# A top-2 mixture-of-experts block on one core: the first expert's second weights in two loads, a reordered front with unmarked row numbers, and seven output buffers for the pairs at the end

## The chip, the core and the metric

One core of a Trainium2 chip runs the whole computation in one launch. The metric is the device time in microseconds (us) of one execution. TensorE is called PE here (PEld is its weight load), VectorE DVE, ScalarE ACT, GpSimd POOL, SyncE SP.

## The reference

The input x has 64 x 64 = 4096 tokens of 256 numbers. Each token is routed to 2 of 8 experts, an expert is a network of three layers, and the weighted sum of its two experts' outputs is added to the token. The gate reads the normed token and a second input per batch row.

```python
var = jnp.mean(x * x, axis=-1, keepdims=True)
xn = rms_w * (x * jax.lax.rsqrt(var + EPS))
gate = xn @ wg_W + wg_b + (genre_embed @ gg_W + gg_b)
gate_w = jax.nn.softmax(gate, axis=-1)
topk_w, topk_i = jax.lax.top_k(gate_w, TOP_K)
cw = jnp.sum(jax.nn.one_hot(topk_i, E, dtype=x.dtype) * topk_w[..., None], axis=-2)
h1 = jax.nn.relu(jnp.einsum('bsh,ehm->bsem', x, W1) + b1)
h2 = jax.nn.relu(jnp.einsum('bsem,emn->bsen', h1, W2) + b2)
out_e = jnp.einsum('bsen,enh->bseh', h2, W3) + b3
x = x + jnp.einsum('bseh,bse->bsh', out_e, cw)
```

E = 8, W1 is 256 x 512, W2 512 x 512 and W3 512 x 256 for each expert, all in float32.

## The kernel before, in words

**The sparse plan.** Only the chosen pairs of token and expert are computed. The pairs of one expert are cut into tiles of 128 rows. POOL fetches the tokens of a tile by number with an indirect DMA, and adds the finished rows to the output by number with another (line 1481, a scatter). A token has two pairs, so a unit's scatters wait until those of the unit before have landed.

**The front.** The first 8 of every 32 tokens (part A) are gated first, so that seven first tiles, one for each of the first seven experts (F = 7), can start early. `first_part` turns tokens with PE (`turn`, `turn_pe` and a copy out of PSUM), multiplies them by the gate's weights (`gates`, `gates_2`), picks the two best experts (`choose`), ranks the pairs, and builds the table of rows `tabA` with one-hot products. A line of DVE turns it into row numbers: `idxA` holds the token's number, and 4096 (a mark beyond the last row) where a tile has an empty place, so that an empty place fetches and writes nothing. `other_loads` issues the loads of the next experts on SP, behind the first gather of rows on POOL. `second_part` goes on with the gate of the other 24 of 32 tokens (part B): more turning, `gates(1, range(4, 8))` with the copy to `gTs` and its turn back (`upright`), then the turn of the first tile's rows (`transpose_x(0)`, line 958, with its copy to `xT`, line 959). Between these stand sums of squares for the norms (`squares`, lines 238 and 240), shared out to ACT and DVE; DVE's come by `some(n)`.

**The head.** `head_step` runs the seven first tiles: layer 1 (line 1090), its relu (1093), layer 2 (1102, 1105), layer 3 (1442). Between its products it finishes the gate of part B (`third_part`, `last_upright`, `norm`, `ranks_of_rest`), plans the rest of the work in `rest()` on DVE, and builds the second table of rows, `idxR`, with 64 one-hot products (`table`, line 649). Row numbers of part B then let POOL gather the rows of the later units.

**The units.** The later tiles are grouped into units of one expert: 4 tiles, 3 tiles or 2 tiles (pairs). Layers 1 and 2 are done by a scheme that takes seven block products in place of eight (class `Fast`, line 1191), layer 3 likewise (`Wide` and, for 3 and 2 tiles, `Duo`, line 1379). Which groups there are is read from the data and picks one of the arms written out beforehand. In the profiled data, nine units of four tiles, four of three and six pairs follow the head. Layer 3 of a unit runs inside the step of the unit behind it, woven into that unit's layers 1 and 2 by hand.

**Outputs.** A unit's finished rows stand in `ys`, 4 buffers of 128 x 256. `y_of` names the buffer: a unit of three or four tiles begins at slot 0, a pair takes slots 0 and 1 or 2 and 3 in turn. ACT (line 1393) and DVE (line 1395) write the quarters of a pair's two buffers in the order ACT, DVE, DVE, ACT, and `send` issues the scatter. A buffer can be written again only when its scatter has landed. The ring `xg` (3 buffers) takes the first tiles' rows, and serves no one after the head but for two outputs.

**Order.** The program is in program order on each engine (a manual schedule): an engine whose next instruction waits holds all behind it. SP's loads are one queue, POOL's gathers and scatters are another.

Of the kernel before, what the change touches and what calls it, by code (L numbers as in the profile page):

```python
# [54 lines left out]
def kernel(  # L55
# [17 lines left out]
    nc = tc.nc  # L73
# [121 lines left out]

    idxA = const.tile([P, E], I32, name="idxA")
    idxR = const.tile([P, NREST], I32, name="idxR")
    ebt = const.tile([P, 1], I32, name="ebt")
# [121 lines left out]
    class Part:  # L320
# [31 lines left out]
        def norm(self, root):  # L352


            var, y, t = (self.t[a] for a in ("var", "y", "t"))
            if root:
                nc.scalar.activation(t, ss[:, self.i0 : self.i1], AF.Sqrt, bias=epsb)
            V.scalar_tensor_tensor(var, ss[:, self.i0 : self.i1], H * EPS, fresh[:, 0, 1:2].to_broadcast([P, self.n]), ALU.add, ALU.add)
            if root:
                V.reciprocal(y, t)  # L360
            else:
                V.tensor_scalar(t.bitcast(I32), var.bitcast(I32), 1, None, ALU.arith_shift_right)
                V.tensor_scalar(y.bitcast(I32), t.bitcast(I32), -1.0, float(0x5F3759DF), ALU.mult, ALU.add)
            n = 1 if root else 3
            for k in range(n):
                V.scalar_tensor_tensor(t, y, -0.5, var, ALU.mult, ALU.mult)
                V.tensor_tensor(t, t, y, ALU.mult)
                V.scalar_tensor_tensor(self.t["rstd"] if k == n - 1 else y, t, 1.5, y, ALU.add, ALU.mult)

        def choose(self, raw, add):  # L370
# [105 lines left out]

    squares_late = []
    left = [NA + i for i in (0, 1, 4, 5, 2, 3, 6, 7)] + list(range(NA + 8, NI))

    def some(n):  # L480
        for _ in range(n):
            squares(left.pop(0), "V")

    def first_part():
# [15 lines left out]
        V.memset(cw8B, 0.0)  # L500
        for k in range(3):
            V.memset(ring(run, [P, H], "xg", 3, k), 0.0)
        V.memset(cgR, 0.0)
# [22 lines left out]
        nc.sync.dma_start(vecs[E * MC : 2 * E * MC, :], b2.rearrange("e (c p) -> (e c) p", p=P))  # L526
        load_weights(0, (0, 1))
        gates_2(((0, 1), (2, 3)), PB[3], ((0, 0), (0, 1), (1, 0), (1, 1)))
# [51 lines left out]
        turn_pe(j0, 0, 3, [TPB - 1])  # L580
        turn_copy(8, "A", 3)
        V.tensor_scalar(sa[:, 0:E], tabA, 0.0, float(NT), ALU.is_equal, ALU.mult)
        V.scalar_tensor_tensor(idxA, tabA, float(OFFA), sa[:, 0:E], ALU.add, ALU.add)
        V.tensor_copy(totA1, pA.tot)
        some(3)

    def other_loads():

        sent = nc.gpsimd.memset(shut, 0.0)

        load_weights(1, (0,))
        tc.add_manual_dep(
            loads[2].ins,
            sent.ins.name,
# [10 lines left out]
    def second_part():  # L605

        j0 = GA + 4
        vps = PB[6][:, 384 : 384 + 2 * E * MC]
        gates(1, range(4, 8))
        nc.scalar.copy(gTs, PB[3])  # L610
        turn_pe(j0, 1, 0)
        turn_pe(j0 + 1, 0, 4)
        turn_copy(9, "A", 0)
        turn_copy(10, "V", 4)
        pA.weights()
        raw = upright(PB[2])
        nc.scalar.copy(graw[:, NA : NA + 4 * TPB, :].rearrange("p (q k) e -> p q k e", q=4), raw)
        turn_pe(j0 + 1, 1, 1)
        turn_copy(11, "A", 1)
        nc.tensor.transpose(vps, vecs, ident[: 2 * E * MC, : 2 * E * MC])  # L620
        V.tensor_copy(vT.rearrange("p l e c -> p (l e c)"), vps)
        gates_2(((8, 9), (10, 11)), PB[7], ((0, 0), (1, 0)))
        squares(left.pop(), "A")
        squares(left.pop(), "A")
        transpose_x(0)
        squares(left.pop(), "A")
        gates_2(((8, 9), (10, 11)), PB[7], ((0, 1), (1, 1)))
        squares_late.extend((left.pop(), left.pop()))
        some(6)

    def third_part():

        nc.scalar.copy(gTs[:, 0:HT], PB[7][:, 0:HT])
        some(len(left))

    def last_upright():
# [256 lines left out]

    def fetch(dst, src, b):

# [3 lines left out]
            in_=src,  # L899
            in_offset=bass.IndirectOffsetOnAxis(ap=index(b), axis=0),  # L900
            bounds_check=NT - 1,
# [10 lines left out]
    def gather(b):  # L912
        fetches.append(fetch(ring(run, [P, H], "xg", 3, b), xrows, b))

# [355 lines left out]
    def y_of(u, k):  # L1270
        if F - 2 <= u < F:
            return ring(run, [P, H], "xg", 3, u + 2)
        return ys[:, slots(u).start + k]

# [250 lines left out]
    def head_step(u):  # L1525
# [3 lines left out]
        for k in range(3 * u, min(3 * u + 3, F)):  # L1529
            gather_cw(k)  # L1530
        layer1(u, {1: ranks_of_rest} if u == 2 else None)
        if u == 0:
# [6 lines left out]
            squares(squares_late.pop(), "A")  # L1539
            layer2(u, {0: lambda: squares(squares_late.pop(), "A"), 1: last_upright, 2: lambda: transpose_x(1)})  # L1540
            stage_1(1)
# [10 lines left out]
        if u == 4:  # L1552
            until("chunk0")
            spread_high[0](2)
            table(GC)
            until("chunk1")
# [15 lines left out]
        elif u == 4:  # L1572
            table(2 * GC)
            until("chunk3")
            layer2(u, {1: lambda: table(3 * GC), 2: table})
        else:
# [431 lines left out]
```

## Time and profile before

| what | value |
|---|---|
| time, median of 3 runs | 441.06 us (439.86 to 442.34) |
| the profiled execution's own time | 441.69 us |
| its span from first to last instruction | 440.0 us |
| PE busy | 431.8 us, 98% |
| DVE, ACT, POOL busy | 350.5, 267.0, 276.6 us |
| mean granted TensorE clock | 0.998 |
| bytes moved by DMA | 96.99 MB, 220 GB/s |

The chain of the work that ended last is 91% PE. Such a kernel is read from PE's idle time: the view of who waited for whom lists the waits of PE, and the table by windows shows in which stretches PE was not busy. A row of the timeline gives the start, the length, the engine, the line and the operation, and in brackets the idle time ahead of it and what ended it. In the view by windows each engine has its busy time and the number of its instructions. In the chain, a row gives start, length and what the time went to.

### The profile page before, as it was taken

To read this page: it belongs to the slowest core of one execution; us is meant where nothing else is said; L and a number is where in the kernel's file an instruction comes from. 1 tells how busy PE (TensorE), PEld (TensorE's weight loads), DVE (VectorE), ACT (ScalarE), POOL (GpSimd) and SP (SyncE) were. 2 spreads that over 40 slices of the span, in tenths; PEclk is the share of its full clock that TensorE was granted. 3 is DMA by queue.
4 is the path that set the end of the run, shared out by engine and by line. 5 is a ranking of instruction groups with operands and counts; after the bars stand their busy time and mean duration, and the time that the engine had idled before them with its cause. 6 is when DMAs were issued, how large, how long until landed. Compare 5 with 4: busy or idle time off the path is not lost.

```text
span 440.0 us, 9508 instructions
## 1 busy us (share of the span) xinstructions
PE 431.8 (98%) x3085; PEld 409.3 (93%) x3085; DVE 350.5 (80%) x894; ACT 267.0 (61%) x787; POOL 276.6 (63%) x233
## 2 busy tenths in 40 slices
PE   9999999999999999999999999999999998999995
PEld 8699999889898999989999999999999998999995
DVE  6899974797868787786868697877877887999982
ACT  6855834646474746565564747475575678577772
POOL 6866335778888767474848483848666677655233
PEclk9999999999999999999999999999999999999999
DMA  8999999899986586674748392939688678878413
GB/s 312 339 345 408 368 324 318 224 334 275 361 199 131 115 230 151 195 170 147 196 127 234 96 253 67 265 93 334 183 256 221 186 210 264 231 242 243 99 20 51
DMA packets 85903, 96.99 MB, mean 220 GB/s; under 512 B 36079, under 2 KB 64850, under 8 KB 85716
## 3 DMA queue, kind: packets, MB, share of 16 engines
q1 hardware_dynamic: 49472, 40.54, 29.0%
q10 hardware_dynamic: 21188, 38.29, 25.6%
q0 software_dynamic: 15184, 17.47, 20.6%
q8 instruction: 26, 0.43, 0.4%
q14 instruction: 33, 0.27, 0.2%
HBM read 80.68 MB, written 20.20 MB: 229 GB/s over the span
## 4 chain that ended last, share of the span: by engine, by line
PE 91%; DMA 5%; issue 2%; DVE 1%; POOL 0%; ACT 0%; POOLq 0%; DVEq 0%
PE pb L1191 56%; PE pb L1320 13%; PE pb L1102 6%; PE pb L1379 5%; DMA out_dram<-ys,idxR 3%; PE pb L1090 3%; PE pb L1442 2%; PE pb L1401 1%; PE pb L649 1%; PE pb L317 1%; DMA xg<-in_x_dram,idxA 1%; PE pb L249 1%; DMA big<-out_dram,idxR 1%; PE pb L280 0%; PE pb L958 0%
## 5 line engine op out<-in xcount | busy, mean ns | idle before, releaser
L1481 POOL DMA_INDIRECT out_dram<-ys,idxR x60 | 99.2, 1654 | 80.8 <-DVE ys L1467 37.3
L896 POOL DMA_INDIRECT cg<-cwdR,idxR x60 | 67.3, 1121 | 18.3 <-issue 17.1
L1248 ACT ACTIVATE hid<-hid,bb 128x256 f32<-128x256 f32 (+9 forms) x158 | 63.4, 451 | 9.3 <-DVE hid L1210 4.4
L1248 ACT ACTIVATE hid<-pb,bb 128x128 f32<-128x128 f32 (+9 forms) x146 | 53.0, 416 | 24.5 <-PE pb L1191 23.5
L1191 PE MATMUL pb<-hid,w2r 128*128 128x128 f32 (+9 forms) x304 | 56.0, 327 | 0.0
L1191 PE MATMUL pb<-hotA,big 128*128 128x128 f32 (+9 forms) x304 | 52.8, 327 | 0.0
L1191 PEld LDWEIGHTS pb<-hotA,big 128*128 128x128 f32 x304 | 47.7, 191 | 2.8
L1191 PEld LDWEIGHTS pb<-hid,w2r 128*128 128x128 f32 x304 | 47.6, 191 | 2.4
L1191 PE MATMUL pb<-mixX,iotx 128*128 128x128 f32 (+9 forms) x228 | 46.5, 327 | 0.0
L896 POOL DMA_INDIRECT xgE<-in_x_dram,idxR x32 | 34.3, 1071 | 18.8 <-DVE ib L827 9.3
L1191 PEld LDWEIGHTS pb<-mixX,iotx 128*128 128x128 f32 x228 | 36.6, 191 | 1.9
L1202 ACT COPY big<-pb 128x256 f32<-128x256 f32 (+9 forms) x39 | 18.8, 483 | 30.4 <-PE pb L1191 29.9
L896 POOL DMA_INDIRECT big<-in_x_dram,idxR x28 | 31.8, 1137 | 8.5 <-issue 7.0
L1200 ACT COPY pb<-pb 128x256 f32<-128x256 f32 (+9 forms) x36 | 16.5, 459 | 25.9 <-PE pb L1191 25.7
L1191 PE MATMUL pb<-xT,w1r 128*128 128x128 f32 (+9 forms) x152 | 31.1, 327 | 0.0
L951 DVE STREAM_TRANSPOSE xT<-gTs 128x256 f32<-128x256 f32 x56 | 29.6, 635 | 0.0
L1191 PE MATMUL pb<-mixB,w2r 128*128 128x128 f32 (+9 forms) x152 | 28.0, 327 | 0.0
L1191 PE MATMUL pb<-mixB,big 128*128 128x128 f32 (+9 forms) x152 | 28.0, 327 | 0.0
L1191 PE MATMUL pb<-hid,big 128*128 128x128 f32 (+9 forms) x152 | 28.0, 327 | 0.0
L1202 ACT COPY q1s<-pb 128x256 f32<-128x256 f32 (+9 forms) x39 | 18.8, 482 | 14.4 <-PE pb L1191 14.4
L1102 PE MATMUL pb<-hid,w2r 128*128 128x128 f32 x224 | 27.3, 276 | 0.0
L1102 PEld LDWEIGHTS pb<-hid,w2r 128*128 128x128 f32 x224 | 26.5, 192 | 0.3
(369 smaller groups left out, 1012.3 us busy)
## 6 DMA issues: line engine op xcount, KB each, us to landing
w2r<-in_L_cond_W_dram ACTq DMA_DIRECT2D x17, 1024.0 KB, 8.7
w2r<-in_L_cond_W_dram SPq DMA_DIRECT2D x9, 1024.0 KB, 12.9
w3r<-in_L_cond_W_dram ACTq DMA_DIRECT2D x17, 512.0 KB, 4.3
w1r<-in_L_cond_W_dram ACTq DMA_DIRECT2D x16, 512.0 KB, 7.5
w1r<-in_L_cond_W_dram SPq DMA_DIRECT2D x10, 512.0 KB, 9.7
w3r<-in_L_cond_W_dram SPq DMA_DIRECT2D x9, 512.0 KB, 11.0
big<-in_x_dram SPq DMA_DIRECT2D x8, 512.0 KB, 5.5
gTs<-scr SPq DMA_DIRECT2D x8, 512.0 KB, 4.7
```

The costliest lines, as they stand in the source:

```text
L896: return nc.gpsimd.indirect_dma_start(out=dst, out_offset=None, in_=src, in_offset=bass.IndirectOffsetOnAxis(ap=index(b), axis=0), bounds_ ...
L951: V.transpose(xT[:, :, s0 + k, :].rearrange("p c (b k) -> p k c b", b=SQ), shs[:, s0 + k].rearrange("p k (a c) -> p k c a", a=SQ),)
L1090: nc.tensor.matmul(ph, lhsT=w1[:, c, ts(m, P)], rhs=cols[:, c, :], start=(c == 0), stop=(c == HC - 1))
L1102: nc.tensor.matmul(ph, lhsT=w2[:, m, ts(n, P)], rhs=hid[0][:, m, 0:BT], start=(m == 0), stop=(m == MC - 1))
L1191: nc.tensor.matmul(bank[:, ts(n, self.w)], lhsT=w[:, c, ts(n, P)], rhs=x[:, c], start=new and n == 0 and c == 0, stop=n == HB - 1 and c == ...
L1200: nc.scalar.copy(self.A, self.U)
L1202: nc.scalar.copy(self.q[(1, 6, 5).index(k)], self.tall(self.X if k == 5 else self.U))
L1248: nc.scalar.activation(out, src, AF.Relu, bias=ww[self.u][1][:, self.l, n : n + 1])
L1320: nc.tensor.matmul(bank[:, ts(j, H // 2)], lhsT=a[:, c, ts(j, P)], rhs=b[:, c], start=new and j == 0 and c == 0, stop=j == 1 and c == HB - ...
L1379: nc.tensor.matmul(bank, lhsT=a[:, c], rhs=b[:, c], start=False, stop=c == HB - 1, skip_group_check=True)
L1442: nc.tensor.matmul(sums(u, k), lhsT=hid[1][:, n, ts(k, BT)], rhs=w3[:, n, :], start=(i == 0), stop=(i == MC - 1))
L1481: add = nc.gpsimd.indirect_dma_start(out=orows, out_offset=bass.IndirectOffsetOnAxis(ap=index(b)[0:n], axis=0), in_=y[0:n], in_offset=None ...
```

## The change

It has three parts.

1. **W2 of the first expert** is loaded in two halves of its columns (`half_of_first`). The first half stands where the whole load stood. The second is issued in `other_loads` and waits for a new array of row numbers, `rowA`.
2. **Unmarked numbers and the front's order.** `rowA` is the table plus an offset, in integers, with no mark: an empty place of a tile fetches some token's row, which is never written out. The gathers of the first tiles use it in place of `idxA`; the scatters and the weights' gathers keep `idxA`. The three memsets of `xg` go. In `second_part` the turns and all gate products come ahead of the first rows' turn; the rows are turned into two PSUM banks, and ACT and DVE copy one half each to `xT`; the upright turn of the gate stands behind them. DVE's squares are dealt 1 + 2 + 6 in place of 3 + 6 ahead of the head, and one of ACT's squares moves into the head's first layer 2. `ranks_of_rest` moves behind the fourth product group of its layer 1, the first 16 one-hot products behind a layer 3, the last 16 behind the fourth group of a layer 2. `norm` carries `z = -0.5 * y * var` along, with the same number of operations.
3. **Seven buffers.** Outputs of the units of two and three tiles go round through the 3 buffers of `xg` and the 4 of `ys`.

```diff
     idxA = const.tile([P, E], I32, name="idxA")
+    rowA = const.tile([P, E], I32, name="rowA")
...
+            n, z = 1 if root else 3, self.t["den"]
+            V.scalar_tensor_tensor(z, y, -0.5, var, ALU.mult, ALU.mult)
             for k in range(n):
-                V.scalar_tensor_tensor(t, y, -0.5, var, ALU.mult, ALU.mult)
-                V.tensor_tensor(t, t, y, ALU.mult)
+                V.tensor_tensor(t, z, y, ALU.mult)
                 V.scalar_tensor_tensor(self.t["rstd"] if k == n - 1 else y, t, 1.5, y, ALU.add, ALU.mult)
+                if k < n - 1:
+                    V.scalar_tensor_tensor(z, t, 1.5, z, ALU.add, ALU.mult)
...
+    def half_of_first(k):
+        h = slice(k * M // 2, (k + 1) * M // 2)
+        return nc.sync.dma_start(w2r[0][:, :, h], W2[0].rearrange("(c p) n -> p c n", p=P)[:, :, h])
...
-        for k in range(3):
-            V.memset(ring(run, [P, H], "xg", 3, k), 0.0)
...
-        load_weights(0, (0, 1))
+        load_weights(0, (0,))
+        half_of_first(0)
...
+        found.append(V.tensor_scalar(rowA, tabA, float(OFFA), None, ALU.add))
         V.tensor_scalar(sa[:, 0:E], tabA, 0.0, float(NT), ALU.is_equal, ALU.mult)
...
-        some(3)
+        some(1)
...
+        later = half_of_first(1)
+        tc.add_manual_dep(
+            later.ins,
+            found[0].ins.name,
...
-        gates(1, range(4, 8))
-        nc.scalar.copy(gTs, PB[3])
         turn_pe(j0, 1, 0)
...
-        pA.weights()
-        raw = upright(PB[2])
-        nc.scalar.copy(graw[:, NA : NA + 4 * TPB, :].rearrange("p (q k) e -> p q k e", q=4), raw)
         turn_pe(j0 + 1, 1, 1)
         turn_copy(11, "A", 1)
         nc.tensor.transpose(vps, vecs, ident[: 2 * E * MC, : 2 * E * MC])
+        gates(1, range(4, 8))
+        gates_2(((8, 9), (10, 11)), PB[7], ((0, 0), (1, 0), (0, 1), (1, 1)))
+        squares(left.pop(), "A")
+        nc.scalar.copy(gTs, PB[3])
+        some(2)
         V.tensor_copy(vT.rearrange("p l e c -> p (l e c)"), vps)
-        gates_2(((8, 9), (10, 11)), PB[7], ((0, 0), (1, 0)))
+        pA.weights()
+        g = ring(run, [P, H], "xg", 3, 0).rearrange("p (r c) -> p c r", c=HC)
+        for c, (bank, eng) in enumerate(((PB[4], nc.scalar.copy), (PB[5], V.tensor_copy))):
+            nc.tensor.transpose(bank[:, 0:BT], g[:, c], ident)
+            eng(xT[:, c, 0, :], bank[:, 0:BT])
+        raw = upright(PB[2])
+        nc.scalar.copy(graw[:, NA : NA + 4 * TPB, :].rearrange("p (q k) e -> p q k e", q=4), raw)
         squares(left.pop(), "A")
-        squares(left.pop(), "A")
-        transpose_x(0)
-        squares(left.pop(), "A")
-        gates_2(((8, 9), (10, 11)), PB[7], ((0, 1), (1, 1)))
-        squares_late.extend((left.pop(), left.pop()))
+        squares_late.extend((left.pop(), left.pop(), left.pop()))
         some(6)
...
-        fetches.append(fetch(ring(run, [P, H], "xg", 3, b), xrows, b))
+        fetches.append(fetch(ring(run, [P, H], "xg", 3, b), xrows, b, rowA[:, b : b + 1]))
...
+        if u >= F and 1 < size(u) < SLOTS:
+            first = next(v for v in range(F, u + 1) if size(v) < SLOTS)
+            n = (turn_of(u, k) - turn_of(first, 0)) % (SLOTS + 3)
+            return ring(run, [P, H], "xg", 3, n) if n < 3 else ys[:, n - 3]
         return ys[:, slots(u).start + k]
...
-        layer1(u, {1: ranks_of_rest} if u == 2 else None)
+        layer1(u, {3: ranks_of_rest} if u == 2 else None)
...
             spread_high[0](2)
-            table(GC)
             until("chunk1")
...
-            layer2(u, {1: lambda: table(3 * GC), 2: table})
+            layer2(u, {1: lambda: table(3 * GC), 3: table})
```

**PE in the front, before.** From the last product of part A's table to the first products of the head. Rows with `big` turn tokens, rows with `wg_sb` are gate products, `gTs` is the gate's upright turn, `vecs` the biases' turn, `xg` the first tile's rows, `w1r` layer 1.

```order
L424 MATMUL pb_74<-incA,ones_105 128x9
L249 MATMUL pb_73<-ident,big 128x128
L265 MATMUL pb_71<-hid_93,wg_sb 32x512 x4
L249 MATMUL pb_68<-ident,big 128x128 x4
L249 MATMUL pb_72<-ident,big 128x128 x4
L299 MATMUL pb_70<-ident,gTs 128x128 x4
L249 MATMUL pb_69<-ident,big 128x128 x4
L620 MATMUL pb_74<-ident,vecs 128x64
L280 MATMUL pb_75<-q1s,wg_sb 32x256 x4
L958 MATMUL pb_72<-ident,xg_212 128x128 x2
L280 MATMUL pb_75<-q1s,wg_sb 32x256 x2
L280 MATMUL pb_75<-mixB,wg_sb 32x256 x2
```

The same stretch of PE now:

```order
L427 MATMUL pb_74<-incA,ones_105 128x9
L250 MATMUL pb_73<-ident,big 128x128
L250 MATMUL pb_68<-ident,big 128x128 x4
L250 MATMUL pb_72<-ident,big 128x128 x4
L250 MATMUL pb_69<-ident,big 128x128 x4
L629 MATMUL pb_74<-ident,vecs 128x64
L266 MATMUL pb_71<-hid_93,wg_sb 32x512 x4
L281 MATMUL pb_75<-q1s,wg_sb 32x256 x6
L281 MATMUL pb_75<-mixB,wg_sb 32x256 x2
L639 MATMUL pb_72<-ident,xg_381 128x128
L639 MATMUL pb_73<-ident,xg_381 128x128
L300 MATMUL pb_70<-ident,gTs 128x128 x4
```

The last four gate products moved ahead of the first rows' turn and the upright turn moved behind it; nothing was added or taken away.

**ACT in the front, before.** Its work from the two squares behind the exponents to the first relus of layer 1 (`hid`). `q1s` and `mixB` are turned tokens, `gTs` and `graw` the gate.

```order
L238 ACTIVATE sqA,ss<-big 128x256 x2
L260 COPY q1s<-pb_73 128x512
L610 COPY gTs<-pb_71 128x512
L260 COPY q1s<-pb_68 128x512
L617 COPY graw<-pb_70 128x128
L260 COPY mixB<-pb_69 128x512
L238 ACTIVATE sqA,ss<-big 128x256 x2
L959 COPY xT<-pb_72 128x2x128
L238 ACTIVATE sqA,ss<-big 128x256
L1093 ACTIVATE hid_93<-pb_68,vT 128x128
```

And now:

```order
L239 ACTIVATE sqA,ss<-big 128x256 x2
L261 COPY q1s<-pb_73 128x512
L261 COPY q1s<-pb_68 128x512
L261 COPY mixB<-pb_69 128x512
L239 ACTIVATE sqA,ss<-big 128x256
L633 COPY gTs<-pb_71 128x512
L640 COPY xT<-pb_72 128x128
L642 COPY graw<-pb_70 128x128
L239 ACTIVATE sqA,ss<-big 128x256
L1114 ACTIVATE hid_93<-pb_68,vT 128x128
```

The copy of the gate `graw` moved from ahead of the rows' copy to behind it, so a copy and a square stand between the rows and the first relu.

**POOL at the end, before.** From the first units of three tiles to the first pairs, in the arm that the profiled data takes. `out_dram<-` are the scatters, `<-in_x_dram` the gathers of rows, `cg` those of weights.

```order
L1481 DMA out_dram<-ys,idxR 4096x256 x3
L896 DMA big<-in_x_dram,idxR 128x256 x2
L896 DMA cg<-cwdR,idxR 128x8 x2
L1481 DMA out_dram<-ys,idxR 4096x256 x3
L896 DMA xgE<-in_x_dram,idxR 128x256 x2
L896 DMA cg<-cwdR,idxR 128x8 x2
L1481 DMA out_dram<-ys,idxR 4096x256 x2
```

The same stretch of POOL now (the last two units of three tiles, then the first pair):

```order
L1506 DMA out_dram<-ys,idxR 4096x256
L1506 DMA out_dram<-xg_381,idxR 4096x256
L1506 DMA out_dram<-xg_382,idxR 4096x256
L917 DMA big<-in_x_dram,idxR 128x256 x2
L917 DMA cg<-cwdR,idxR 128x8 x2
L1506 DMA out_dram<-xg_383,idxR 4096x256
L1506 DMA out_dram<-ys,idxR 4096x256 x2
L917 DMA xgE<-in_x_dram,idxR 128x256 x2
L917 DMA cg<-cwdR,idxR 128x8 x2
L1506 DMA out_dram<-ys,idxR 4096x256 x2
```

The order of the scatters is as it was; only the buffers that they read have changed, and the first pair's two no longer are those of the unit ahead of it.

More of the change, by code (lines that the diff above doesn't have):

```diff
@@ L363, in norm @@
                 V.tensor_scalar(y.bitcast(I32), t.bitcast(I32), -1.0, float(0x5F3759DF), ALU.mult, ALU.add)
-            n = 1 if root else 3
+            n, z = 1 if root else 3, self.t["den"]
+            V.scalar_tensor_tensor(z, y, -0.5, var, ALU.mult, ALU.mult)
             for k in range(n):
-                V.scalar_tensor_tensor(t, y, -0.5, var, ALU.mult, ALU.mult)
-                V.tensor_tensor(t, t, y, ALU.mult)
+                V.tensor_tensor(t, z, y, ALU.mult)
                 V.scalar_tensor_tensor(self.t["rstd"] if k == n - 1 else y, t, 1.5, y, ALU.add, ALU.mult)
+                if k < n - 1:
+                    V.scalar_tensor_tensor(z, t, 1.5, z, ALU.add, ALU.mult)
         def choose(self, raw, add):
@@ L474, in load_weights @@
             loads.append(nc.sync.dma_start(dst, src))
-    squares_late = []
+    squares_late, found = [], []
     left = [NA + i for i in (0, 1, 4, 5, 2, 3, 6, 7)] + list(range(NA + 8, NI))
@@ L584, in first_part @@
         V.tensor_copy(totA1, pA.tot)
-        some(3)
+        some(1)
     def other_loads():
         sent = nc.gpsimd.memset(shut, 0.0)
+        later = half_of_first(1)
+        tc.add_manual_dep(
+            later.ins,
+            found[0].ins.name,
+            mybir.DependencyInfo(mybir.DependencyClass.Sync, mybir.DependencyReason.DATA),
+            reason="the first tile's rows are found first",
+        )
         load_weights(1, (0,))
         tc.add_manual_dep(
-            loads[2].ins,
+            loads[1].ins,
             sent.ins.name,
@@ L634, in third_part, with late_ones @@
         some(len(left))
+    def late_ones():
+        squares(squares_late.pop(), "A")
+        last_upright()
     def last_upright():
@@ L892, in index, with fetch @@
         return idxA[:, b : b + 1] if b < F else idxR[:, b - F : b - F + 1]
-    def fetch(dst, src, b):
+    def fetch(dst, src, b, at=None):
         return nc.gpsimd.indirect_dma_start(
@@ L899, in fetch @@
             in_=src,
-            in_offset=bass.IndirectOffsetOnAxis(ap=index(b), axis=0),
+            in_offset=bass.IndirectOffsetOnAxis(ap=index(b) if at is None else at, axis=0),
             bounds_check=NT - 1,
@@ L1539, in head_step @@
             squares(squares_late.pop(), "A")
-            layer2(u, {0: lambda: squares(squares_late.pop(), "A"), 1: last_upright, 2: lambda: transpose_x(1)})
+            layer2(u, {0: lambda: squares(squares_late.pop(), "A"), 1: late_ones, 2: lambda: transpose_x(1)})
             stage_1(1)
```

## Prediction

> **What bounds the kernel now.** I read the table by windows first, then the list of PE's waits. In the windows the first numbers are the stretch and its length, then PE's busy time; behind PEclk stand the share of the DMA engines and GB/s.
>
> ```profile
> 16.60:21.00 4.40, 4.15 (x44) 2.52 (x36) 3.52 (x18) 3.75 (x11) 3.86 (x6) 1.00 0.77 247
> 21.00:75.00 54.00, 54.00 (x470) 52.70 (x467) 43.44 (x164) 30.21 (x86) 28.21 (x27) 1.00 1.02 363
> ...
> 362.00:378.00 16.00, 14.42 (x128) 14.17 (x127) 13.22 (x36) 10.76 (x39) 11.04 (x9) 1.00 0.79 218
> ```
>
> ```profile
> PE pb L1379 <- DVE ys L1395: 1.6, 1, 1.6
> PE pb L317 <- PEq L1994: 0.8, 1, 0.8
> PE pb L418 <- DVE d2A L413: 0.3, 1, 0.3
> PE pb L958 <- DMA xg<-in_x_dram,idxA: 0.2, 1, 0.2
> ```
>
> PE sets the time: through the whole head, 21 to 75 us, it has no idle time, and these four are all the waits that the list has for it, 2.9 us together. A change that leaves PE's products as they are can win only there, and at the two ends. This one touches two: the 1.6 us of line 1379 and the 0.2 us of line 958. So the gain has a ceiling of about 2 us, and what else the change moves can only keep or lose it.
>
> **Part 3, the seven buffers.** One row of the chain of waits (start, length), then three of the timeline, show the large wait.
>
> ```profile
> 363.52 10.31 DMA out_dram<-ys,idxR
> ```
>
> ```profile
> 371.63 0.37 ACT L1393 ACTIVATE ys<-pb,cw 128x128 f32<-128x128 f32 x1
> 373.96 0.35 DVE L1395 SCALAR_TENSOR_TENSOR ys<-pb,cw,big 128x128 f32<-128x128 f32 x1 [2.06 <-DMA out_dram<-ys,idxR]
> 374.37 0.71 PE L1379 MATMUL pb<-prB,hid 128*128 128x128 f32 x4 [1.58 <-DVE ys L1395]
> ```
>
> This is the first pair. Its second buffer is slot 1, which the unit of three tiles ahead of it also used; that scatter was issued at 363.52 and took 10.31 us to land. DVE held its write until 373.96, and PE's next product for layer 3 writes the PSUM bank that this DVE operation reads. With seven buffers the first pair's places are two `ys` slots last written two and three units earlier, so this wait goes whole: -1.58 us. The wait does not come back a unit later, since seven buffers are at least two units deep. No operation is added.
>
> What is late next is POOL. A unit's scatters also wait for the landing of the unit's before, and the buffers do not change that. Rows of POOL's scatters, then of the DVE writes that two of them follow, then a scatter's landing at the end from the chain:
>
> ```profile
> 365.91 1.53 POOL L1481 DMA_INDIRECT out_dram<-ys,idxR  x1 [0.81 <-ACT ys L1425]
> ...
> 375.71 1.63 POOL L1481 DMA_INDIRECT out_dram<-ys,idxR  x1 [2.32 <-DVE big L1152]
> 377.64 1.57 POOL L1481 DMA_INDIRECT out_dram<-ys,idxR  x1 [0.31 <-ACT big L1202]
> ...
> 388.15 1.64 POOL L1481 DMA_INDIRECT out_dram<-ys,idxR  x1 [3.46 <-ACT ys L1393]
> ```
>
> ```profile
> 374.56 0.34 DVE L1395 SCALAR_TENSOR_TENSOR ys<-pb,cw,big 128x128 f32<-128x128 f32 x1
> 387.01 0.35 DVE L1395 SCALAR_TENSOR_TENSOR ys<-pb,cw,big 128x128 f32<-128x128 f32 x1
> ```
>
> ```profile
> 425.14 4.00 DMA out_dram<-ys,idxR
> ```
>
> The scatters at 375.71 and 388.15 start 0.81 and 0.79 us behind the end of DVE's write, the same lag twice, so the rows set them and not the landing. It follows that the scatter of 365.91 landed within 9.8 us. With rows 1.6 us earlier, the first pair's scatter may now meet that landing and wait up to 1.6 us. PE does not feel it, because the buffers are free. It is given back at the pace of the pairs: 12.44 us from one pair's first scatter to the next's (388.15 less 375.71), against 1.93 us between a pair's two scatters plus a landing; at 9.8 us the cycle needs 11.7, so 0.7 us are made up per pair and the delay is gone by the third of six. At the end, where the last unit reads the output back, the landing is 4.00 us. I take 0, bounded by 0 and +1.6 us.
>
> **Parts 1 and 2, the front.** First the rows on the row numbers and the gather, then PE's and ACT's rows up to the first relus; the last two of ACT are means by group in this stretch. Below these stand the gather's row of the chain and the window of 18 to 19 us.
>
> ```profile
> 15.90 0.17 DVE L582 TENSOR_SCALAR sa<-pb 128x8 f32<-128x8 f32 x1 [0.57 <-PE pb L424]
> 16.11 0.17 DVE L583 SCALAR_TENSOR_TENSOR idxA<-pb,sa 128x8 int32<-128x8 f32 x1
> 16.56 1.13 POOL L896 DMA_INDIRECT xg<-in_x_dram,idxA  x1 [0.52 <-DVE totA L584]
> 17.92 0.60 PE L299 MATMUL pb<-ident,gTs 128*128 128x128 f32 x4
> 18.35 0.60 PE L249 MATMUL pb<-ident,big 128*128 128x128 f32 x4
> 18.55 0.27 ACT L617 COPY graw<-pb 128x128 f32<-128x128 f32 x1 [0.29 <-PE pb L299]
> 19.09 0.64 PE L280 MATMUL pb<-q1s,wg_sb 128*32 128x256 f32 x8
> 19.97 0.50 PE L958 MATMUL pb<-ident,xg 128*128 128x128 f32 x2 [0.25 <-DMA xg<-in_x_dram,idxA]
> 20.97 2.05 PE L1090 MATMUL pb<-xT,w1r 128*128 128x128 f32 x16
> 21.72 1.71 ACT L1093 ACTIVATE hid<-pb,vT 128x128 f32<-128x128 f32 x4 [0.43 <-PE pb L1090]
> ```
>
> ```profile
> L238 ACT ACTIVATE sqA<-big 128x256 f16<-128x256 f32 x4 | 1.7, 418 | 0.1
> L238 ACT ACTIVATION_READ_ACCUMULATOR sqA<-big 128x1 f32 x3 | 0.6, 189 | 0.0
> ```
>
> ```profile
> 16.56 3.37 DMA xg<-in_x_dram,idxA
> ```
>
> ```profile
> 18.00:19.00 1.00, 1.00 (x10) 0.83 (x8) 0.81 (x2) 0.54 (x3) 1.00 (x1) 1.00 0.57 176
> ```
>
> The gather. `rowA` stands where line 582 stood, so it is there at 16.07 in place of 16.28. The gather starts 0.28 us behind its numbers now, so at 16.35, 0.21 earlier, and with the same 3.37 us its rows are there at 19.72.
>
> PE. Its products are the same, in another order. It was through with the first four gate products at 19.73 (19.09 + 0.64). Now the other four stand ahead of the rows too (+0.64 at most), and the upright turn does not (-0.43, from 17.92 to 18.35): PE comes to the rows at 19.9 at the latest; I take 19.8. So a landing at 19.72 costs no wait, and an earlier one wins nothing.
>
> Behind the rows, PE turns two halves, and the upright turn (0.43) covers the copies; layer 1 can start some 0.75 us later, where it took 1.00 (19.97 to 20.97). But ACT now has the gate's copy (0.27) and a square (0.42 + 0.19) between the rows and the relus: 0.22 for the two turns (the upright turn's four take 0.43), 0.43 for the upright turn, 0.20 until ACT sees it (18.55 against 17.92 + 0.43), and 0.88 make 1.7 us. Relus start at 19.8 + 1.7 = 21.5, against 21.72. I take -0.2 us; the bounds are -0.45 (PE's gain alone) and +1.0 (rows late, see the second rival).
>
> The second half of W2 is moved past nothing on SP but its own wait; behind it on SP stand the next expert's loads, which already waited for POOL's instruction behind the gather and so lose nothing. The three memsets ran on DVE ahead of its first wait for x, and the steps of `norm` stay nine: 0.
>
> DVE now waits for the rows with its half of the copy, and the squares of part B queue behind it. They resumed at 19.56 and now resume at 20.55, behind the copy. Who waits for them is PE's `ranks_of_rest`, and behind that the row table; rows of the first square, of the end of that chain, and of the first unit's gather and turn:
>
> ```profile
> 19.56 0.41 DVE L240 CUSTOM_DVE_ANT_0 sqV<-big 128x256 f16<-128x256 f32 x1
> ...
> 34.35 0.17 DVE L413 TENSOR_TENSOR d2B<-cw8B,prB 128x24 f32<-128x24 f32 x1
> 35.15 0.18 PE L418 MATMUL pb<-incB,tri 128*128 128x8 f16 x1
> ...
> 61.06 1.00 POOL L896 DMA_INDIRECT xgE<-in_x_dram,idxR  x1 [9.30 <-DVE ib L827]
> ...
> 75.20 0.64 PE L964 MATMUL pb<-ident,xgE 128*128 128x128 f32 x4
> ```
>
> PE came 0.6 us behind that chain (34.52 to 35.15), and moving the ranks behind two more product groups adds 0.9: cover 1.3 for a delay of 1.0. Without that cover it would cost the difference, up to 0.4. The table's last products move 0.9 later, and 14 us lie between the gather and its use. Both 0.
>
> **Sum.** 441.69 for the profiled execution, -1.58 and -0.2, is 439.9. The median of the runs shown lies 0.63 below that execution, so the forecast is **439.3 us**, 0.4% under 441.06. About 0.5% (2.2 us) is what a measurement of this kernel can tell from no change, so the forecast counts as no change.
>
> **The rivals.**
>
> *The scatters keep the time.* If landings among the pairs stay near 10.31 us, a pair's cycle is 12.2 of 12.44 us, 0.2 are made up per pair, and the last unit's read-back comes 0.8 us late or more of the 1.58: 440.1, and with nothing made up 440.9. For it speaks 10.31; against it that 375.71 shows a landing under 9.8 and the end one of 4.00. [...] Chance 0.12.
>
> *The rows come late.* The half load now falls into the very microseconds in which the gather's rows move: the window shows the DMA engines busy for 0.57 there. At the rate that this share gives, 176 / 0.57 = 310 GB/s, the half's 0.52 MB take 1.7 us and the rows' 0.13 MB 0.42. If the engines alternate, the rows land 0.42 later, at 20.1, and the front wins nothing; if the half goes first, up to 1.2 is lost against the forecast: 439.5 to 440.5. [...] Chance 0.15.
>
> *The wait was smaller in the other runs.* It hangs on one landing that outlasted the need by 2.06 us; with half of it the forecast is 440.1 or more. Chance 0.13.
>
> *Slower: the second half is what layer 2 waits for.* One load's landing, and the chain's row on the third group of the first layer 2:
>
> ```profile
> w3r<-in_L_cond_W_dram SPq DMA_DIRECT2D x1, 512.0 KB, 12.0
> ```
>
> ```profile
> 25.08 0.89 PE pb L1102 x8
> ```
>
> Issued at 16.1, the half is needed at 24.9. With 12.0 us, as this load of its size took, it lands at 28.1; PE stands 3.2 us, and the time is 442.5. It decides from 8.8 us on and turns the sum from 10.6. Against it: nothing is queued ahead of it. Chance 0.05.
>
> *More.* Both terms at their bounds, -2.06 (all that DVE idled there) and -0.45: 438.6. Chance 0.1.
>
> **Numbers.** The forecast has 0.45, with its own range 438.6 to 440.1. The range 438.2 to 441.2 adds the second and third rivals and the first. Faster by over 0.5% is the last case and a third of the forecast's share, with the spread of the medians: 0.27. Slower by over 0.5% is part of the slow rival: 0.04. The rest, 0.69, is no change.
>
> **What would show it.** Right: line 1379 has no wait for DVE; seen from then on, PE has no idle time to the last unit; the gather starts near 16.35 and the first relu near 21.5. Wrong: POOL's scatters among the pairs start over 1 us behind their rows up to the last unit; PE waits for `xg` by more than 0.25; a wait of line 1102 for `w2r`, or of the ranks for DVE.

## The result, and the profile after

The changed kernel takes 443.7 us (median of 8 runs, 441.95 to 444.2), the kernel before 441.12 (8 runs, 439.86 to 442.34): a ratio of 1.0063, interval 1.0049 to 1.0077. It is 2.6 us slower where 1.8 us less was forecast, and 2.5 us above the upper end of the range. Medians here and below are of all runs; the ratios, and the counts by clock, leave out runs over 1.5% above the fastest of their kernel.

First PE's waits in the changed kernel, the first two of four; the other two are of 0.2 us each.

```profile
PE pb L639 <- DMA xg<-in_x_dram,rowA: 2.0, 1, 2.0
PE pb L318 <- PEq L2018: 0.9, 1, 0.9
```

The 1.6 us of the first pair (line 1379 before) are gone. In their place stands a wait of 2.0 us for the first rows, 0.25 before. The chain of waits (start, length) shows the rows and what follows them:

```profile
16.98 5.08 DMA xg<-in_x_dram,rowA
22.06 0.04 issue
22.11 0.50 PE pb L639 x2
22.61 0.46 PE pb L300 x4
23.07 3.45 PE pb L1111 x16
26.52 1.84 PE pb L1123 x16
28.36 0.22 PE pb L293 x2
28.58 0.89 PE pb L1123 x8
```

The gather took 5.08 us to land, 3.37 before, and so PE's turn of the rows starts at 22.11 in place of 19.97. But the third group of layer 2 starts at 28.58, where it was 25.08: 3.5 us late, not 2.1. The rest lies in one row: the 16 products of layer 1 took 3.45 us, and 1.98 in the same view of the kernel before:

```profile
21.04 1.98 PE pb L1090 x16
```

The table by windows of the changed kernel says why (behind the length PE's busy time; the column ahead of the DMA share is the granted clock):

```profile
20.00:22.00 2.00, 0.06 (x4) 0.00 (x0) 0.00 (x0) 0.00 (x0) 1.82 (x4) 1.00 0.77 230
22.00:22.75 0.75, 0.65 (x5) 0.65 (x6) 0.04 (x1) 0.22 (x1) 0.53 (x1) 1.00 1.10 328
22.75:23.00 0.25, 0.25 (x4) 0.21 (x3) 0.25 (x2) 0.04 (x1) 0.25 (x2) 0.78 0.75 266
23.00:26.25 3.25, 3.25 (x17) 3.25 (x17) 3.01 (x16) 1.77 (x6) 1.15 (x2) 0.50 1.05 370
26.25:26.50 0.25, 0.25 (x4) 0.25 (x4) 0.25 (x1) 0.00 (x0) 0.00 (x0) 0.90 1.02 385
```

PE has work from 22.11 on, but its clock is granted at 0.50 over a stretch: 0.78 and 0.90 at its edges put it from 22.89 to 26.30, 3.41 us, in which PE does half the work, a loss of 1.7 us. So the loss at the head is the wait and the clock, less some 0.3 us that the new order gains behind the rows (shown further down). At the end the forecast came in:

```profile
362.00:378.00 16.00, 15.95 (x166) 15.43 (x165) 14.17 (x38) 11.62 (x43) 10.89 (x9) 1.00 0.69 202
```

14.42 before. The span went from 440.0 to 442.0 us: 3.5 at the head, less the 1.6 here.

My theory was then: the second half of W2 makes the rows late, and PE's idle time halves its clock. The rival: the unmarked numbers or the new order are what delays the rows. A second question was why 2.6 us are lost and not 2.0.

### The profile page after: what moved, and what is told of

It reads as the page before. It is cut to its first block, busy times and chain, and to the rows that moved or that the text cites. A ratio compares the mean times of both kernels' runs of the same rounds, so it can differ in the third digit from the quotient of the medians.

```text
span 442.0 us, 9504 instructions
## 1 busy us (share of the span) xinstructions
PE 433.3 (98%) x3085; PEld 411.2 (93%) x3085; DVE 350.5 (79%) x893; ACT 266.4 (60%) x787; POOL 275.4 (62%) x233
## 4 chain that ended last, share of the span: by engine, by line
PE 92%; DMA 4%; ACT 1%; issue 1%; DVE 1%; POOLq 0%; POOL 0%; DVEq 0%; ACTq 0%
PE pb L1212 57%; PE pb L1345 13%; PE pb L1404 6%; PE pb L1123 6%; PE pb L1111 3%; PE pb L1467 2%; DMA xg<-in_x_dram,rowA 1%; PE pb L1426 1%; DMA big<-in_x_dram 1%; DMA out_dram<-ys,idxR 1%; PE pb L670 1%; PE pb L250 1%; ACT hid L1269 1%; DMA big<-out_dram,idxR 1%; PE pb L1474 0%
## 5 line engine op out<-in xcount | busy, mean ns | idle before, releaser
L1506 POOL DMA_INDIRECT out_dram<-ys,idxR x48 | 80.3, 1674 | 62.8 <-DVE ys L1492 37.3
L917 POOL DMA_INDIRECT cg<-cwdR,idxR x60 | 66.3, 1106 | 18.3 <-issue 16.8
L1506 POOL DMA_INDIRECT out_dram<-xg,idxR x12 | 19.3, 1604 | 15.5 <-DVE hotA L1195 4.7
```

The costliest lines, as they stand in the source:

```text
L917: return nc.gpsimd.indirect_dma_start(out=dst, out_offset=None, in_=src, in_offset=bass.IndirectOffsetOnAxis(ap=index(b) if at is None els ...
L1506: add = nc.gpsimd.indirect_dma_start(out=orows, out_offset=bass.IndirectOffsetOnAxis(ap=index(b)[0:n], axis=0), in_=y[0:n], in_offset=None ...
```

## The experiments: which part loses the time

Four kernels of one factor each, timed beside each other and the kernel before.

**One load, all else as changed.**

```diff
-        load_weights(0, (0,))
-        half_of_first(0)
+        load_weights(0, (0, 1))
...
-        later = half_of_first(1)
```

> Once more the changed kernel with the second weights in one load, beside its neighbours of one factor each. Theory A: rows in time, clock 1.00 from 20 to 30 us. What the seven buffers are worth is open: 1.6 us if every execution had the wait of the first pair, and some 0.8 by the run with nine products of constants (its head was 2.0 us late and its time 1.2 us over before, so 0.8 came back). So before - 0.8 (439.7) to before - 1.8 (438.7).

Measured: 440.23 us against 440.99 for the kernel before; ratio 0.9964, 0.993 to 0.9998. In its profile the gather landed in 3.75 us, PE waited 0.7 us for the rows, and the clock was 1.00 from 19 to 28 us.

**The seven buffers alone**, on the kernel before (`y_of` as in the change):

> Once more the kernel before with the seven buffers alone. Theory A with the full wait: before - 1.6 us. If the wait of the first pair stands in part of the executions alone (the run with the split load alone had none, with the old buffers): before - 0.8 us or less.

Measured: 440.21 us; ratio 0.9983, 0.9948 to 1.0017.

**The changed kernel again:**

> The changed kernel itself, as the yardstick of this row of four: before + 2.6 us, rows late by 2 us, the clock at half for one or two stretches of 3.4 us. If the length of the half-rate stretch changes from execution to execution: times in two groups, 1.7 us apart.

Measured: 443.1 us; ratio 1.0032, 1.0002 to 1.0062, a smaller loss than the first time, with intervals that overlap. The times do stand in two groups, by the mean clock of the run: 441.3, 441.5 and 441.9 at 0.998, seven from 442.4 to 443.8 at 0.993 to 0.996; the means lie 1.6 us apart.

**The front alone**: the edit of one load, and `y_of` as before the change.

> The new order of the front with the unmarked numbers, one load and the old buffers: the front by itself. The prediction's term of the front says before - 0.2 us; theory B (order or unmarked numbers lose the time) says before + 3.5 us; a new order that costs something of its own, such as PE waiting for ACT behind the rows: up to before + 1 us.

Measured: 440.29 us; ratio 0.9981, 0.9949 to 1.0013. Its chain has the gather at nearly its old landing, and layer 1 at full pace:

```profile
16.39 0.15 DVE rowA L587
...
16.82 3.56 DMA xg<-in_x_dram,rowA
20.39 0.04 issue
20.43 0.50 PE pb L631 x2
20.94 0.44 PE pb L300 x4
21.37 1.85 PE pb L1103 x16
```

Behind the rows the new order does gain what was forecast. Here are ACT's first relus, from the timeline:

```profile
21.98 1.65 ACT L1106 ACTIVATE hid<-pb,vT 128x128 f32<-128x128 f32 x4
```

They start 1.55 us behind PE's turn of the rows (20.43), where it was 1.75 before (19.97 to 21.72).

**The split alone**, on the kernel before:

```diff
-        load_weights(0, (0, 1))
+        load_weights(0, (0,))
+        half_of_first(0)
...
+        later = half_of_first(1)
```

The late half waits for the instruction of line 582.

> The kernel before with the split load alone: the first half early, the second on SP behind the DVE instruction of line 582 (no unmarked numbers, no new order, no seven buffers). Theory A: the half moves in the gather's microseconds and ahead of it, so the gather lands 4.7 to 5.1 us behind its issue in place of 3.4, PE waits for the rows by 1.5 to 2 us, its clock is halved for some 3.4 us behind that wait, and the time is 1.5 + 1.5 to 2.0 + 1.7 us over before: +3.0 to +3.7 us. Theory B (the order or the unmarked numbers are what delays the rows): the gather lands 3.4 us behind its issue, the time is as before.

Measured: 443.85 us against 440.51; ratio 1.0061, 1.0036 to 1.0086. Old order, marked numbers, old buffers, and the whole loss is there. PE waited 2.2 us for the rows; the chain:

```profile
16.70 5.28 DMA xg<-in_x_dram,idxA
...
23.73 3.71 PE pb L1102 x16
27.45 2.38 PE pb L1114 x16
```

So the split load is the loss, and the rival is out. What the other two parts are worth, each alone, can't be told from nothing: both intervals hold 1.

Two of these had run earlier, with two more told of below, on a chip on which each kernel, the one before too, took 454 to 467 us, and PE stood for 2 to 3 us in several places for which the profile names no cause. From them I take the ratios and the head alone.

> The changed kernel with the first expert's second weights in one load again, as before the change; the reordered front, the unmarked numbers and the seven buffers stay. Theory A (the second half's bytes move ahead of the gather's and make the rows late; the idle time of PE then halves its clock): the gather lands about 3.4 us behind its issue as before the change, PE waits for the rows under 0.3 us, the granted clock stays 1.00 from 20 to 28 us, and both losses go, 2.0 and 1.7 us: 443.7 - 3.7 = 440.0, or, counted from the kernel before, 441.1 - 1.6 - 0.2 = 439.3; so 439.3 to 440.0. Theory B (the unmarked numbers or the new order of the front make the rows late, the loads have no part in it): landing 5 us behind its issue, PE waits 2 us, 443.7.

Ratio 0.9975, 0.9948 to 1.0002; landing 3.69 us, wait 0.7 (more than the 0.3 expected), clock 1.00 from 19 to 28 us.

> The kernel before with the seven buffers alone. If the wait of the first pair goes whole, as the changed kernel's list of waits says: PE busy over 15.9 of 16 us from 362 to 378, 441.1 - 1.6 = 439.5. If POOL's landings give it back later: 440.1 to 441.1, with POOL's scatters among the pairs over 1 us behind their rows.

Ratio 0.9984, 0.9943 to 1.0024.

**Why the buffers are worth less than 1.6 us.** The front alone has the old buffers, and yet its window has no wait:

```profile
362.00:378.00 16.00, 16.00 (x144) 15.96 (x144) 14.50 (x41) 11.64 (x44) 11.79 (x9) 1.00 0.83 232
```

Its timeline has the scatter that reads slot 1, and DVE's first write for the pair; the last row, from the view of `ys`, has landing times of the scatters in 355 to 380 us:

```profile
362.43 1.58 POOL L1494 DMA_INDIRECT out_dram<-ys,idxR  x1 [0.31 <-ACT pb L1213]
372.13 0.35 DVE L1408 SCALAR_TENSOR_TENSOR ys<-pb,cw,big 128x128 f32<-128x128 f32 x1
DMA to landing us min/median/max: 4.6/8.7/8.9
```

The scatter went out 1.09 us earlier than the 363.52 of the profile before and landed within 8.9 us, by 371.33, ahead of the write. The split alone had no wait there either (PE busy 16.00 of 16 us). Three kernels told of below, with POOL held up at the front, have the old buffers too: the list of PE's waits has the wait for the one with eight copies, and not for those with two and four:

```profile
PE pb L1379 <- DVE ys L1395: 1.8, 1, 1.8
```

So it stands in two of six profiled executions with the old buffers, the one that the forecast was made from among them. Why POOL sends that scatter earlier in one execution than in another was not tried.

## The experiments: idle time and the clock

**Products of constants in the gap**, 18, then 9, on the changed kernel:

```diff
+        one = nc.const_aps.tensor(1.0, [P, P], F32)
+        for _ in range(18):
+            nc.tensor.matmul(PB[5][:, 0:P], lhsT=one, rhs=one, start=True, stop=True)
         g = ring(run, [P, H], "xg", 3, 0)...
```

> The changed kernel with 18 products of constants more on PE, in the gap ahead of the turn of the first rows, which nothing reads; the computation is the same. Theory A: the rows are still late by 2 us, PE does not idle over 0.5 us, the clock stays 1.00, and layer 1 of the first unit takes 2.0 us again in place of 3.45: 443.7 - 1.7 = 442.0. If the clock falls for another reason than the idle time (the DMA traffic, the change of work at the first expert): half rate near 23 us again, 443.7.

This was among the runs on that other chip. The products took 4.21 us, twice the gap, so its ratio (1.009, 1.0055 to 1.0125) has the excess in it; the clock stayed 1.00 and layer 1 took 1.85 us.

> The changed kernel with half as many products of constants in the gap (9 in place of 18, which were two passes each and took 4.21 us, twice the gap). Theory A: the rows are as late as in the changed kernel, PE idles under 0.5 us, the clock stays 1.00, layer 1 of the first unit takes 2.0 us: 1.7 us under the changed kernel, so before + 0.9 us. If the clock falls nonetheless: before + 2.6 us.

Measured: 441.69 us against 440.51; ratio 1.0029, 1.0002 to 1.0057. The gather took longer than in any other profile whose chain has it (5.55 us at most there), PE was kept busy until 0.4 us before the rows, the clock was 1.00 from 19.25 to 30 us, and layer 1 ran at full pace:

```profile
16.29 5.64 DMA xg<-in_x_dram,rowA
21.98 0.50 PE pb L642 x2
...
22.92 1.85 PE pb L1114 x16
```

So with rows as late as these, useless work on PE kept the clock: 1.00 at the head in both profiles, and a mean of 0.997 or more in each of the eleven runs that the ratio of the second counts. What that is worth in time is not settled: the change itself was not timed beside this one, and its two measurements, 1.0063 and 1.0032 against 1.0029 here, put it between 1.5 and 0.1 us.

**The gap without the half**: the kernel before, with POOL busy ahead of the first gather (eight copies; then two and four).

```diff
+        nc.gpsimd.tensor_copy(pB.w[:, 0, :], idxA)
+        for _ in range(8):
+            nc.gpsimd.tensor_copy(pB.w[:, 0:NA, :], pA.ohe[:, 1].rearrange("p e i -> p i e"))
         gather(0)
```

> The kernel before, in which POOL makes nine small copies that nothing reads ahead of the first gather, so that the rows come some 2 us later with the loads as they were: the idle time of PE by itself, without the half load. Theory A: PE waits about 2 us for the rows, its clock falls to half for some 3.4 us behind that, and the time rises by the wait and 1.7 us, +3.7 us. If the half load's traffic or the changed order is what halves the clock: clock 1.00, and the time rises by the wait alone, +2 us.

Measured: 447.34 us against 440.51; ratio 1.0133, 1.01 to 1.0166. POOL's copies took longer than I had reckoned, so PE waited 3.7 us. The clock by windows:

```profile
23.50:23.75 0.25, 0.00 (x0) 0.00 (x0) 0.22 (x3) 0.00 (x0) 0.24 (x1) 0.54 0.95 328
23.75:30.25 6.50, 6.04 (x30) 4.91 (x31) 3.15 (x14) 2.46 (x9) 4.13 (x7) 0.50 0.96 320
30.25:30.50 0.25, 0.25 (x4) 0.25 (x3) 0.00 (x0) 0.25 (x2) 0.00 (x0) 0.81 1.01 393
```

Half rate from 23.52 to 30.35, 6.83 us or twice 3.41, with no half load in flight. 3.45 us more wait and 3.4 for the clock make 6.85. The medians differ by 6.83, but that they meet so closely is luck: the five runs that the ratio counts spread from 445.07 to 448.83 us, the ratio makes 5.9 us, and the profiled run also had the wait of line 1379.

> The kernel before with POOL's useless copies ahead of the first gather, two and a cast in place of eight: eight took 3.39 us and PE waited 3.7 us, so two make PE wait 1.0 to 1.2 us. If a wait of that length is too short to halve the clock: clock 1.00 throughout, before + 1.2 us, in one group of times. If it halves it in part of the executions, by where the wait falls in a stretch of 3.4 us: two groups, 1.7 us apart.

Measured: 442.6 us against 440.42; ratio 1.0035, 1.0014 to 1.0057. PE waited 1.45 us, and even so the profiled execution lost its clock:

```profile
21.25:22.00 0.75, 0.73 (x10) 0.47 (x10) 0.68 (x5) 0.19 (x1) 0.73 (x1) 1.00 1.08 410
22.00:22.25 0.25, 0.25 (x8) 0.00 (x0) 0.25 (x1) 0.25 (x2) 0.25 (x1) 0.81 0.70 250
22.25:25.50 3.25, 3.25 (x19) 3.18 (x16) 3.01 (x15) 1.28 (x5) 2.68 (x7) 0.50 0.96 290
25.50:25.75 0.25, 0.25 (x4) 0.25 (x4) 0.25 (x2) 0.16 (x1) 0.25 (x1) 0.86 0.94 369
```

Five of eleven runs have a mean clock of 0.993 or 0.994 (442.8 to 443.5 us), six of 0.997 or more (441.05 to 442.4).

> The same with four copies: PE waits 1.9 to 2.1 us, as in the changed kernel, with no half load in flight. If the wait alone halves the clock: before + 2.0 us in executions that keep the clock (0.997 and above) and + 3.7 us or + 5.4 us in those that lose one or two stretches of 3.4 us at half; the changed kernel had 3 of 10 in the upper clock. If the half load's traffic has a part in it: clock 1.00, before + 2.0 us, in one group.

Measured: 444.41 us; ratio 1.0071, 1.0045 to 1.0098. PE waited 2.29 us in the profile; seven of nine runs lost clock (443.9 to 445.4 us at 0.993 to 0.996), two did not (441.9 and 442.9).

So idle time of PE is enough to halve the clock, without the half load, over 3.41 us or twice that, and by the runs' mean clocks the odds rise with the gap: 5 of 11 at 1.45 us, 7 of 9 at 2.3, 5 of 5 at 3.7. (The gap is that of the profiled execution. Of the kernel before, timed beside the first two, 2 of 19 runs have 0.996 or less.)

## The experiments: how the half delays the rows

**The half behind POOL's instruction after the gather:**

```diff
-            found[0].ins.name,
+            sent.ins.name,
```

> The changed kernel with the second half held until POOL's instruction behind the first gather, as the next expert's loads are, about 1.2 us later than the row numbers. Theory A: the gather's rows are ahead of the half again, so PE waits under 0.3 us for the rows, the clock stays 1.00; the half, issued near 18, lands by 22 to 24, in time for layer 2 near 24.5: 439.3 to 440.0. Should the half come too late, PE waits in front of the third group of layer 2 by up to 1 us: 441. Theory B: rows late by 2 us as in the changed kernel, 443.7.

On that other chip: ratio 0.9968, 0.9931 to 1.0005. No wait for the rows, clock 1.00 from 19 to 28 us.

> The changed kernel with the second half behind POOL's instruction after the first gather, timed beside the other three. Theory A: the rows land about 3.4 us behind the gather's issue, no wait for them, clock 1.00, and the 1.6 us of the seven buffers are all that is left: before - 1.6 to - 1.8 us. Theory B: before + 2.6 us as the changed kernel.

Measured: 441.05 us against 440.51; ratio 1.0006, 0.9986 to 1.0025. The rows were in time, but the profiled execution has a wait for weights, which stands from 45.57 to 47.29 us:

```profile
PE pb L1123 <- DMA w2r<-in_L_cond_W_dram: 1.7, 1, 1.7
```

That is the W2 of the fourth expert. SP issued it at 29.95, 2.25 us later than in the front alone (27.70), which has no such wait. That the half, now ahead of it on SP, made it late is argued and not tested; and this execution took 445.3 us, 4.3 over the median, so the wait need not stand in the others.

**Another size**: a quarter or three quarters late in place of a half.

```diff
-        h = slice(k * M // 2, (k + 1) * M // 2)
+        h = slice(0, 3 * M // 4) if k == 0 else slice(3 * M // 4, M)
```

> The changed kernel with a quarter of the second weights (0.26 MB) behind the row numbers in place of a half. If the DMA engines move what was asked for first before the gather's rows, the delay goes with its bytes: the half made the gather land 5.1 to 5.6 us behind its issue where one load has 3.6 to 3.8, so 1.8 us more; a quarter then gives 0.9 more, 4.6 us. If engines alternated between the two queues, the rows' 0.13 MB would be slowed by as much again as they take alone, whatever the size behind: 4.0 us.

Landing 4.63 us; PE waited 1.6; clock whole (0.997 over the run); 441.55 us in one run against 440.42.

> The same with three quarters (0.79 MB) behind the row numbers. By bytes: 2.7 us more than one load, so the gather lands 6.4 us behind its issue, PE waits over 3 us and its clock is halved for two stretches of 3.4 us. By alternation: 4.0 us, as for a quarter.

Landing 4.92 us, less than with the half; PE waited 1.9; one stretch at half rate (0.994 over the run); 442.81 us in one run. Both expectations miss: the landing does not go with the size. But the first rows come later with it. Packets per queue in stretches of 0.5 us; q0 is the gathers', q1 SP's loads. The kernel before, at 18 and 18.5 us (gather issued at 16.56):

```profile
q0 software_dynamic: 7, 0.03, 25.4%
q1 hardware_dynamic: 7, 0.01, 7.3%
...
q0 software_dynamic: 34, 0.09, 59.0%
q1 hardware_dynamic: 13, 0.04, 21.4%
```

The changed kernel at 18.5, 19 and 19.5 us (gather issued at 16.98):

```profile
q1 hardware_dynamic: 181, 0.19, 104.9%
...
q1 hardware_dynamic: 182, 0.18, 104.2%
...
q0 software_dynamic: 16, 0.06, 89.6%
q1 hardware_dynamic: 71, 0.06, 40.9%
```

With three quarters, at 20 and 20.5 us (gather issued at 16.92):

```profile
q1 hardware_dynamic: 129, 0.20, 105.3%
...
q1 hardware_dynamic: 83, 0.11, 58.3%
q0 software_dynamic: 29, 0.09, 46.4%
```

By stretches of 0.2 us the first rows move 1.7 us behind the issue in the kernel before, 1.9 with a quarter, 2.0 to 2.5 with the half, 3.6 with three quarters, each time as the late load's last packets thin out. Until then the load has the engines to itself: from 18.5 to 19.5 us of the changed kernel q1 has 363 packets and q0 none. From the first to the last packets of the late load the profile counts 510 to 530 packets of q1 at each size, some 32 for each of 16 engines. Behind that point the rows' last packets trail: until 21.9 us with the half, 21.5 with three quarters, 19.7 before the change, while the next loads of q1 run. So in these profiles the rows begin where the late load ends. Size is only a part of that: the load began to move at 17.7 us in the changed kernel and, but for some 25 packets, at 18.7 with three quarters, though the two gathers were issued 0.06 us apart. What sets the landing after that stays open.

**The late half in pieces:**

```diff
+        step = w2r[0].shape[1] if k == 0 else w2r[0].shape[1] // 2
+        for c in range(0, w2r[0].shape[1], step): ...dma_start(w2r[0][:, c : c + step, h], ...)
```

> The changed kernel with the late half asked for in two loads of 0.26 MB, one behind the other on SP (some 0.37 us apart); bytes and place are the same. In the runs so far the first rows moved just when the late load's last did, 1.9 to 3.6 us behind the gather's issue, in place of 1.7 to 1.8 with nothing in their way. If the engines take turns between the queues by whole loads (each engine's share of one load, 32 rows of the half, at once): the first rows move behind the first piece, 1.8 to 2.1 us behind the issue, with the second piece behind them. If what was asked for earlier goes first whatever its form: behind both pieces, 2.4 to 2.6 us, as in the changed kernel.

440.78 us in one run; landing 4.54 us, PE waited 1.5, clock whole (0.999 over the run). The rows moved between the pieces, 1.9 us behind the issue. But this does not tell turns from order: SP's second issue took 1.39 us, and the first 0.37, so the second piece came when the rows were moving already.

> The same in four loads of 0.13 MB, of which SP asks for the last two behind the gather. By turns of whole loads: first rows 1.7 to 2.0 us behind the issue, PE waits for the rows 0.5 to 1.2 us, the clock stays whole in most executions: some 1.5 us under the changed kernel, before + 0.5 to + 1.2 us. By order of asking: behind the first two pieces alone, so 1.9 to 2.1 us behind the issue, and the same time; the tail of the rows, 2 us in the changed kernel, shows then whether sharing alone makes them late.

441.52 us against 441.6; ratio 0.9962, 0.9919 to 1.0005. Landing 3.23 us, wait for the rows 0.2, clock whole (0.999 over the profiled run), and in the profiled execution 0.5 us of wait for the fourth expert's W2. Again SP's issues were spread, over 2.5 us, so that the gather passed between the first piece and the second. Turns or order of asking: open.

## Why the prediction was wrong

- **The step that failed** is the gather's: "with the same 3.37 us its rows are there at 19.72". It took 5.08, and PE, at the rows by 20.1, stood for 2.0 us. (The issue was 0.63 us later than forecast as well, 16.98 for 16.35; but the start of `rowA` lies anywhere between 15.86 and 16.96 us in the profiles that have it, and PE's work ahead of the rows moves with it.) The danger was seen, as the rival *the rows come late*, but with 0.15 and at too low a price, by two errors. One end of it had the engines alternate (+0.42), which no run shows; in the trace the half went ahead, 457 packets of q1 from 17.7 to 19.5 us and none of q0, and the first rows moved 0.8 us later behind the issue (2.5 for 1.7). Its other end, "if the half goes first, up to 1.2 is lost", covers that much, but took the rows to move as fast as before once they begin; by stretches of 0.2 us they took 2.4 us to the last packet (19.5 to 21.9) in place of 1.4 (18.3 to 19.7). Why they trail is open.
- **A term was missing**: the clock. PE's idle time was priced at its length. It costs another 1.7 us in most executions (7 of 8 runs, then 7 of 10, have a mean clock of 0.996 or less), so the rival's 440.5 would have had to be some 3.5 us over a kernel with its rows in time. The stretches at half rate were 3.41 or 6.83 us long, and a gap of 1.45 us was enough for one.
- **The seven buffers**: the mechanism was right (no wait in line 1379's place, none later, PE busy 46.00 of 46 us from 378 to 424 us), the size was not: 1.58 us in the profiled execution, about 0.8 by the medians (440.21 against 440.99), with an interval that holds no change. The rival *the wait was smaller in the other runs* was the case, at 0.13, in another form: in the profiles the wait is there whole (1.6 and 1.8 us) or not at all (four of six).
- **POOL's landings** gave nothing back, as taken. Also right: the gather starts 0.28 us behind the end of `rowA` (16.70 to 16.98); no wait of the ranks; no wait of layer 2 for the second half in the changed kernel's profile, so the slower rival was the wrong one.
- **The front's 0.2 us** were not seen in the time. They are there behind the rows (relus 1.55 us behind the turn in the front alone, 1.75 before; the third group of layer 2 4.85 behind it, 5.11 before), and the numbers do lead to the gather sooner (0.43 us from the start of `rowA`'s instruction, 16.39 to 16.82 in the front alone, where line 582's start to the gather took 0.66, 15.90 to 16.56), but landings of 3.56 to 3.75 us with one load, and waits of 0.5 to 0.7 us for the rows, used that up.
- **The median as the yardstick**: the forecast was made against one execution with a wait that others did not have. The change removes it where it stands, and adds 3.5 us, or 1.8 where the clock holds, to each. That answers the second question: 3.5 less about 0.8 is 2.7, near the 2.6 of the medians.

Of all that was timed, only the version with one load, the new front and the seven buffers has an interval under 1, and barely: 0.9964 of the kernel before (0.993 to 0.9998). It can't be told from the buffers alone or the front alone, whose medians are the same within 0.1 us, nor from the four pieces (0.9962, with an interval that holds 1).

## What to carry to other kernels

A load moved into the microseconds of a small transfer that PE waits for can hold it back until the load's last bytes are through, as it did here (first rows 2.5 us behind the issue with the half, 1.7 without), and not just share with it; move it behind the small transfer's issue, or leave it early. Price a new idle stretch of PE at its length and, at the lengths tried here, count in a chance of 1.7 us more for the clock (5 of 11 runs at 1.45 us, 7 of 9 at 2.3). Before a wait is entered in a sum, look whether a second execution has it: one profile shows one landing.

## What the hardware showed that was not expected

- PE's clock was halved after a gap of 1.45 us between stretches of dense work. In all seven profiles that show it, it lasted 3.41 us or 6.83, whatever the gap (1.45 to 3.7 us), from an instant that differed (21.67 to 23.52 us). In the 3.41 us that ended where the clock fell, PE was busy for 1.97 us with the gap of 1.45, for 1.38 in the changed kernel; in the front alone, whose clock held, it was busy for 2.89 of the 3.42 us to 22.89. The length of the gap alone does not decide it: with 1.5 us (two pieces) and 1.6 (a quarter), in one profile each, the clock held. What does was not found.
- A second DMA issue on SP, right behind the first and beside POOL's gather, took 1.39 us where the first took 0.37. The cause is open: other issues of SP in the kernel before took up to 5.12 us.
- The gather's landing without a load in its way was 2.88 to 2.91 us (the three gap kernels; in the long gap the DMA engines stood at 0.00 ahead of it) against 3.37 in the kernel before.
